# Attention and a selective scan on one core: the product with B on VectorE, the sum over states in quarters of the array

## The chip, the core and the metric

The kernel runs on one core of one Trainium2 chip. The core has a TensorE (matrix products, written to PSUM), a VectorE, a ScalarE (functions such as Exp), a GpSimd and 16 DMA engines fed by queues, among them that of SyncE. Each engine works through its own instructions in order, and semaphores hold one back until what it reads is there. The metric is the device time of the whole program in microseconds; lower is better.

## What is computed

The input x has 16 images of 256 channels and 32 x 32 positions, in float32. Two layers follow each other, each added to its input.

- The first normalizes in 16 groups, adds a position embedding, and runs self-attention over the 1024 positions with 4 heads of 32, then a feed-forward step.
- The second normalizes again and computes from 256 channels an inner u of 512 channels, with a gate z, and per position 64 values B and 64 values C. Its core is a recurrence over the 1024 positions, for each of 512 channels and 64 states:

```
dA = exp(delta * A)              # delta: [512, 1024], A: [512, 64]
h  = dA * h + (delta * u) * B    # one h for each channel and state
y  = sum over the 64 states of h * C
```

  Then y + u * D is multiplied by silu(z), projected to 256 channels, and multiplied by a sigmoid gate from a convolution over three positions.

There are 16 x 512 x 64 recurrences of 1024 steps, and every one is computed in full.

## The kernel before

The 512 channels of the scan are 4 blocks of 128, so channels lie on partitions and positions along the row. 16 images with 4 blocks each make 64 blocks of 64 states. `scan_layer` runs them one after the other. For each state n it

1. copies row n of B and row n of C from DRAM to all 128 partitions (tiles bt and ct, two buffers each, issued by SyncE, L429 and L430),
2. multiplies du = delta * u by bt on GpSimd into dub (four buffers, L432),
3. computes the decays da = exp(delta * A) on ScalarE in two halves of 512 positions, into two PSUM buffers (L436),
4. runs the recurrence on VectorE, half by half, in place in dub; the second half starts from the last element of the first (L440),
5. multiplies by ct on VectorE (L443),
6. sums over states on TensorE: a product with the identity that adds dub to y in PSUM, in two halves (L445). A float32 product appears in the trace as two passes, each with its own load of weights.

After the 64 states, y is taken from PSUM on VectorE (L455), the z products and silu follow (L462 to L470), and the next block begins with `deltas` (L397 to L416): a product, then a softplus in which ScalarE and VectorE take turns, then du.

Everything else is side work for the neighbouring images: the attention of the next one and the inputs of its scan, the gate and output of the last one. They are generators, and after every second state `scan_layer` takes one step of them (L450). Only the first image's attention and inputs run ahead of the first scan. `query_key` makes queries and keys for one head. In the attention of a head the scores are made twice: once to find the row maxima (L268, with a VectorE maximum of each at L271), and once transposed, with the maximum as an extra row, for Exp and the product with V (L290, L294, L295).

A scheduler orders the instructions of each engine from its own estimate of their durations and from priorities in the order of the program; the program's order is therefore not quite the engine's. Buffers come from pools: a tile with so many buffers waits, when it comes round again, for the last reader of the old content. PSUM has 8 banks: three for products of all kinds (mm), one for the attention's result (accp), two for y, two for the decays.

Of the kernel before, what the change touches and what calls it, by code (L numbers as in the profile page):

```python
# [10 lines left out]
F32 = mybir.dt.float32  # L11
AF = mybir.ActivationFunctionType
ALU = mybir.AluOpType
AX = mybir.AxisListType
PSUM = bass.MemoryType.PSUM
DRAM = bass.MemoryType.DRAM

P = 128
C = 256
KC = C // P  # L20
# [26 lines left out]
def attention_then_scan_kernel(  # L47
# [21 lines left out]
    def pool(name, bufs, **kw):  # L69
        return ctx.enter_context(tc.tile_pool(name=name, bufs=bufs, **kw))  # L70
# [9 lines left out]
    ptp = pool("ptp", 3)  # L80
    small = pool("small", 2)
    scan = pool("scan", 2)
    dubs = pool("dubs", 4)
    bcd = pool("bcd", 2, space=DRAM)
    mm = pool("mm", 3, space=PSUM)
    accp = pool("accp", 1, space=PSUM)
    yps = pool("yps", 1, space=PSUM)
    daps = pool("daps", 2, space=PSUM)


    vec = const.tile([P, NV], F32, name="vec")
# [2 lines left out]
    def col(name, i=0, n=1):  # L94
        o, w = _COLS[name]
        assert i + n <= w
        return vec[:, o + i : o + i + n]
# [21 lines left out]

    ident = const.tile([P, P], F32, name="ident")  # L120
    make_identity(nc, ident)
    avg = const.tile([P, P], F32, name="avg")
    nc.vector.memset(avg, 1.0 / C)
    eps = const.tile([P, 1], F32, name="eps")
# [5 lines left out]
    def psum(name, dims=P):  # L130
        return mm.tile([P, HL], F32, name=name, tag="mm")[:dims]
# [4 lines left out]
    def hwork(name):  # L136
        return half.tile([P, HL], F32, name=name, tag="half")

    def hs(h):
        return ts(h, HL)  # L140
# [69 lines left out]
    def attention_layer(b):  # L210
# [32 lines left out]
            yield  # L243


        def query_key(h):
            qa, ka = work("qa"), work("ka")
            for hf in range(2):
                ps = psum("qk_ps", 2 * DH)
                for k in range(KC):  # L250
                    nc.tensor.matmul(  # L251
                        ps, wqk_s[:, k, ts(h, 2 * DH)], xn[k][:, hs(hf)],
                        start=(k == 0), stop=(k == KC - 1),
                    )
                nc.scalar.activation(qa[:DH, hs(hf)], ps[:DH], AF.Copy, scale=DH**-0.5)
                nc.scalar.copy(ka[:DH, hs(hf)], ps[DH:])
            nc.gpsimd.memset(ka[DH : DH + 1], 1.0)
            return qa, ka

        ao = sums = None  # L260
        for h in range(HEADS):
            qa, ka = query_key(h)
            yield
            mx = small.tile([P, NJ, 2], F32, name="mx", tag="mx")
            for c in range(NJ):
                for hf in range(2):
                    s = psum("s_ps")
                    nc.tensor.matmul(  # L268
                        s, qa[:DH, ts(c, P)], ka[:DH, hs(hf)], start=True, stop=True
                    )  # L270
                    nc.vector.tensor_reduce(mx[:, c, hf : hf + 1], s, AX.X, ALU.max)  # L271
                yield
            neg = small.tile([P, NJ], F32, name="neg", tag="neg")
            nc.vector.tensor_reduce(neg, mx, AX.X, ALU.max, negate=True)
            for hf in range(2):
                row = psum("row_ps", 1)
                for c in range(NJ // 2):
                    i = hf * (NJ // 2) + c
                    nc.tensor.matmul(
                        row[:, ts(c, P)], neg[:, i : i + 1], ident, start=True, stop=True  # L280
                    )
                nc.scalar.copy(qa[DH : DH + 1, hs(hf)], row)
            yield
            if h == 0:
                ao, sums = work("ao"), work("sums")
            for hf in range(2):
                av = accp.tile([P, HL], F32, name="av", tag="av")[: 2 * DH]
                for j in range(NJ):
                    s = psum("st_ps")
                    nc.tensor.matmul(  # L290
                        s, ka[: DH + 1, ts(j, P)], qa[: DH + 1, hs(hf)], start=True, stop=True
                    )
                    pt = ptp.tile([P, HL], F32, name="pt", tag="pt")
                    nc.scalar.activation(pt, s, AF.Exp)  # L294
                    nc.tensor.matmul(  # L295
                        av, vv[j // (NJ // 2)][:, j % (NJ // 2), h, :], pt,
                        start=(j == 0), stop=(j == NJ - 1),
                    )
                    if j % 2:
                        yield  # L300
                nc.scalar.copy(ao[ts(h, DH), hs(hf)], av[:DH])
                nc.scalar.copy(sums[ts(h, DH), hs(hf)], av[DH:])
            yield
        for hf in range(2):
            nc.vector.reciprocal(sums[:, hs(hf)], sums[:, hs(hf)])  # L305
# [89 lines left out]


    def deltas(b, d):  # L397
        delta = dels.tile([P, L], F32, name="delta", tag="delta", bufs=2)
        for hf in range(2):
            ps = psum("d_ps")  # L400
            nc.tensor.matmul(
                ps, wdt_s[:, ts(d, P)], state[b]["dt"][:, hs(hf)], start=True, stop=True
            )
            o = delta[:, hs(hf)]
            e, s, l = hwork("sp_e"), hwork("sp_s"), hwork("sp_l")
            nc.scalar.activation(e, ps, AF.Abs, bias=col("dt_b", d))
            nc.scalar.activation(e, e, AF.Exp, scale=-1.0)
            nc.vector.tensor_scalar(s, e, 1.0, None, ALU.add)
            nc.scalar.activation(l, s, AF.Ln)  # L409
            nc.vector.scalar_tensor_tensor(e, s, 1.0, e, ALU.subtract, ALU.subtract)  # L410
            nc.vector.tensor_tensor(l, l, e, ALU.subtract)
            nc.scalar.activation(o, ps, AF.Relu, bias=col("dt_b", d))  # L412
            nc.vector.tensor_tensor(o, o, l, ALU.add)
        du = dels.tile([P, L], F32, name="du", tag="du", bufs=2)
        nc.vector.tensor_tensor(du, delta, state[b]["us"][d], ALU.mult)
        return delta, du  # L416

# [2 lines left out]
    def scan_layer(b, side):  # L420
        us, rows = state[b]["us"], state[b]["rows"]
        for d in range(ND):
            blocks = (d,)
            delta, du = deltas(b, d)
            ys = [yps.tile([P, L], F32, name="y", tag="y")]
            for n in range(NS):
                bt = scan.tile([P, L], F32, name="bt", tag="bt")
                ct = scan.tile([P, L], F32, name="ct", tag="ct")
                nc.sync.dma_start(bt, rows[n : n + 1].partition_broadcast(P))  # L429
                nc.sync.dma_start(ct, rows[NS + n : NS + n + 1].partition_broadcast(P))  # L430
                dub = dubs.tile([P, L], F32, name="dub", tag="dub")
                nc.gpsimd.tensor_tensor(dub, du, bt, ALU.mult)  # L432
                at = d * NS + n
                for hf in range(2):
                    da = daps.tile([P, HL], F32, name="da", tag="da")
                    nc.scalar.activation(  # L436
                        da, delta[:, hs(hf)], AF.Exp, scale=a_neg[:, at : at + 1]
                    )
                    before = dub[:, HL - 1 : HL] if hf else 0.0
                    nc.vector.tensor_tensor_scan(  # L440
                        dub[:, hs(hf)], da, dub[:, hs(hf)], before, ALU.mult, ALU.add
                    )
                nc.vector.tensor_tensor(dub, dub, ct, ALU.mult)  # L443
                for hf in range(2):
                    nc.tensor.matmul(  # L445
                        ys[0][:, hs(hf)], ident, dub[:, hs(hf)],
                        start=(n == 0), stop=(n == NS - 1),
                    )
                if n % 2:
                    next(side, None)  # L450

            for i, d in enumerate(blocks):
                for hf in range(2):
                    u = us[d][:, hs(hf)]
                    nc.vector.scalar_tensor_tensor(  # L455
                        u, u, col("D", d), ys[i][:, hs(hf)], ALU.mult, ALU.add
                    )
            for d in blocks:
                for hf in range(2):
                    ps = psum("z_ps")  # L460
                    for k in range(KC):
                        nc.tensor.matmul(  # L462
                            ps, win_s[:, k, ds(DI + d * P, P)],
                            state[b]["xp"][:, k, ds(1 + hf * HL, HL)],
                            start=(k == 0), stop=(k == KC - 1),
                        )
                    z = hwork("z")
                    nc.scalar.activation(z, ps, AF.Silu)
                    u = us[d][:, hs(hf)]
                    nc.vector.tensor_tensor(u, u, z, ALU.mult)  # L470


    def gate_and_store(b):
# [103 lines left out]
```

## Time and profile before

| | |
|---|---|
| median of 2 runs | 21276.39 us (21272.64 and 21280.14) |
| the profiled execution: time, span | 21280.14 us, 21278.3 us |
| TensorE busy, granted clock | 75%, 0.847 |
| VectorE busy | 91% |
| ScalarE busy | 41% |
| GpSimd busy | 50% |
| DMA | 4366 MB, 205 GB/s |

"Busy" is the time in which an engine runs an instruction, its waiting for a port inside the instruction included. A group row of the profile gives line, engine, operation, tiles, shapes and count, then busy time in us and the mean duration of one in ns, then the idle time of the engine just before these instructions and what ended most of it. A row of the timeline gives start and duration in us, engine, line, operation and count; x2 means that two instructions in a row are merged. PEld is TensorE's load of weights, which runs beside its products.

### The profile page before, as it was taken

To read this page: it belongs to the slowest core of one execution; us is meant where nothing else is said; L and a number is where in the kernel's file an instruction comes from. 1 tells how busy PE (TensorE), PEld (TensorE's weight loads), DVE (VectorE), ACT (ScalarE), POOL (GpSimd) and SP (SyncE) were. 2 spreads that over 40 slices of the span, in tenths; PEclk is the share of its full clock that TensorE was granted. 3 is DMA by queue.
4 is the path that set the end of the run, shared out by engine and by line. 5 is a ranking of instruction groups with operands and counts; after the bars stand their busy time and mean duration, and the time that the engine had idled before them with its cause. 6 is when DMAs were issued, how large, how long until landed. Compare 5 with 4: busy or idle time off the path is not lost.

```text
span 21278.3 us, 126145 instructions
## 1 busy us (share of the span) xinstructions
PE 15872.9 (75%) x30080; PEld 5818.2 (27%) x30080; DVE 19310.4 (91%) x15491; ACT 8732.8 (41%) x12360; POOL 10710.9 (50%) x4486
## 2 busy tenths in 40 slices
PE   8877868777687776877768777786777868778656
PEld 2222222232322323222222222322223222232212
DVE  4998998989989899898999989999998998989998
ACT  3443444434444344443444434444444344434433
POOL 1554554555545455555555455555554554545554
PEclk7888888888888888888888888888888888888878
DMA  1666656666666666666666566665665656656666
GB/s 64 215 211 203 219 199 207 212 201 214 206 211 209 200 213 205 212 204 203 213 208 215 201 208 213 207 217 201 213 204 201 224 200 206 208 203 223 202 221 210
DMA packets 1199439, 4366.25 MB, mean 205 GB/s; under 512 B 132817, under 2 KB 135249, under 8 KB 1198689
## 3 DMA queue, kind: packets, MB, share of 16 engines
q1 hardware_dynamic: 1182816, 4299.45, 60.4%
q0 software_dynamic: 15872, 58.73, 0.7%
q8 instruction: 236, 3.87, 0.1%
q14 instruction: 515, 4.21, 0.1%
HBM read 4332.47 MB, written 25.17 MB: 205 GB/s over the span
## 4 chain that ended last, share of the span: by engine, by line
DVE 41%; issue 22%; DMA 9%; PE 7%; ACT 6%; POOL 6%; DVEq 0%; SPq 0%; POOLq 0%; ACTq 0%
DVE dub L440 27%; DVE dub L443 10%; POOL dub L432 6%; DMA bt<-rows 5%; DMA ct<-rows 4%; PE y L445 4%; ACT da L436 3%; PE av L295 1%; DVE u L370 1%; DVE xn L204 0%; PE st_ps L290 0%; ACT L436 0%; DVE sums L305 0%; DVE xn L205 0%; ACT L409 0%
## 5 line engine op out<-in xcount | busy, mean ns | idle before, releaser
L432 POOL TENSOR_TENSOR dub<-du,bt 128x1024 f32<-128x1024 f32 x4096 | 10393.4, 2544 | 9821.0 <-DMA bt<-rows 4216.4
L445 PE MATMUL y<-dub,ident 128*128 128x512 f32 x16384 | 10075.2, 752 | 4576.3 <-DVE dub L443 4568.0
L440 DVE TENSOR_TENSOR_SCAN dub<-da,dub 128x512 f32<-128x512 f32 x8192 | 10070.1, 1241 | 956.9 <-POOL dub L432 705.4
L436 ACT ACTIVATE da<-delta,a_neg 128x512 f32<-128x512 f32 x8192 | 5642.5, 691 | 10511.2 <-DVE dub L440 10499.4
L443 DVE TENSOR_TENSOR dub<-dub,ct 128x1024 f32<-128x1024 f32 x4096 | 7095.2, 1734 | 110.7 <-DMA ct<-rows 66.0
L445 PEld LDWEIGHTS y<-dub,ident 128*128 128x128 f32 x16384 | 3424.0, 228 | 10665.2 <-DVE dub L443 7546.2
L268 PE MATMUL s_ps<-ka,qa 32*128 32x512 f32 x2048 | 1188.0, 688 | 129.1 <-DVE mx L271 127.9
L295 PE MATMUL av<-pt,vv 128*64 128x512 f32 x2048 | 1180.2, 682 | 134.6 <-ACT pt L294 134.6
L290 PE MATMUL st_ps<-qa,ka 33*128 33x512 f32 x2048 | 1104.2, 643 | 36.8 <-ACT delta L412 26.8
L294 ACT ACTIVATE pt<-st_ps 128x512 f32<-128x512 f32 x1024 | 593.8, 594 | 755.7 <-PE st_ps L290 751.9
L271 DVE TENSOR_REDUCE mx<-s_ps 128x1 f32<-128x512 f32 x1024 | 680.5, 665 | 210.3 <-PE s_ps L268 209.4
L268 PEld LDWEIGHTS s_ps<-ka,qa 32*128 32x128 f32 x2048 | 362.8, 204 | 971.4 <-issue 401.9
L290 PEld LDWEIGHTS st_ps<-qa,ka 33*128 33x128 f32 x2048 | 336.4, 192 | 781.1 <-issue 716.7
L295 PEld LDWEIGHTS av<-pt,vv 128*64 128x64 f32 x2048 | 242.4, 151 | 1024.0 <-ACT da L436 446.2
L482 PEld LDWEIGHTS g_ps<-wg_s,xp 128*128 128x128 f32 x1536 | 395.2, 327 | 80.2 <-issue 51.8
L482 PE MATMUL g_ps<-wg_s,xp 128*128 128x256 f32 x1536 | 408.3, 413 | 4.1 <-ACT delta L412 4.1
L436 ACT ACT_TABLE_LOAD x299 | 383.6, 1283 | 5.2
L370 DVE SCALAR_TENSOR_TENSOR u<-up,vec,u 128x1024 f32<-128x1024 f32 x192 | 319.7, 1672 | 7.5 <-ACT u L364 7.3
L493 PE MATMUL m_ps<-wo_s,u 128*128 128x256 f32 x1024 | 280.6, 418 | 33.6 <-DVE u L470 33.6
L197 PE MATMUL ln_v<-ln_sq,avg 128*128 128x512 f32 x256 | 167.4, 757 | 182.8 <-ACT ln_sq L196 182.8
L384 PE MATMUL x_ps<-u,wx_s 128*128 128x512 f32 (+1 forms) x512 | 279.4, 651 | 23.8 <-ACT u L376 23.7
L251 PE MATMUL qk_ps<-xn,wqk_s 128*64 128x512 f32 x512 | 284.8, 659 | 0.0
(111 smaller groups left out, 6881.3 us busy)
## 6 DMA issues: line engine op xcount, KB each, us to landing
bt<-rows SPq DMA_DIRECT2D x4096, 512.0 KB, 4.8
ct<-rows SPq DMA_DIRECT2D x4096, 512.0 KB, 4.2
X<-in_x_dram POOLq DMA_DIRECT2D x16, 1024.0 KB, 6.9
tok<-in_pos_dram POOLq DMA_DIRECT2D x32, 512.0 KB, 6.6
out_dram<-X POOLq DMA_DIRECT2D x32, 512.0 KB, 5.2
rows<-bc POOLq DMA_DIRECT2D x16, 512.0 KB, 3.9
win_s<-in_w_in_dram SPq DMA_DIRECT2D x1, 1024.0 KB, 14.9
wg_s<-in_w_gate_dram SPq DMA_DIRECT2D x1, 768.0 KB, 16.4
```

The source lines that it names most:

```text
L268: nc.tensor.matmul(s, qa[:DH, ts(c, P)], ka[:DH, hs(hf)], start=True, stop=True)
L271: nc.vector.tensor_reduce(mx[:, c, hf : hf + 1], s, AX.X, ALU.max)
L290: nc.tensor.matmul(s, ka[: DH + 1, ts(j, P)], qa[: DH + 1, hs(hf)], start=True, stop=True)
L294: nc.scalar.activation(pt, s, AF.Exp)
L295: nc.tensor.matmul(av, vv[j // (NJ // 2)][:, j % (NJ // 2), h, :], pt, start=(j == 0), stop=(j == NJ - 1),)
L370: nc.vector.scalar_tensor_tensor(u, up[:, t : t + L], col("conv_w", d * CONV + t), u, ALU.mult, ALU.add)
L432: nc.gpsimd.tensor_tensor(dub, du, bt, ALU.mult)
L436: nc.scalar.activation(da, delta[:, hs(hf)], AF.Exp, scale=a_neg[:, at : at + 1])
L440: nc.vector.tensor_tensor_scan(dub[:, hs(hf)], da, dub[:, hs(hf)], before, ALU.mult, ALU.add)
L443: nc.vector.tensor_tensor(dub, dub, ct, ALU.mult)
L445: nc.tensor.matmul(ys[0][:, hs(hf)], ident, dub[:, hs(hf)], start=(n == 0), stop=(n == NS - 1),)
L482: nc.tensor.matmul(ps[:, ts(q, C)], st["xp"][:, k, ds(first + t, P, 4)], wg_s[:, k, t, :], start=(i == 0), stop=(i == 3 * KC - 1),)
```

## The change

- The product with B goes from GpSimd to VectorE, from du and bt into hh, a tile with four buffers.
- The decays go to SBUF, whole, in one ScalarE instruction of 1024; the scan is one instruction of 1024, the product with C as before.
- The sum over states is made for two states at once, in 64 x 64 quarters of TensorE's array: eight products, of two channel halves i and two states j, and two halves of positions. Channel half i of state j is added to y4[i], partitions 64j on. At the end of a block ScalarE copies the four parts of y4 to SBUF, and a product with `fold` (two 64 x 64 identities above each other, in one half of the columns) adds both states' parts and puts the channel halves in place.
- PSUM: the decays' two banks go to the second y tile.
- The buffers of delta and du go from two to one.
- The attention takes two heads at a time: their queries and keys lie at partitions 0 and 64, and their products with V write the two halves of the rows of one PSUM bank. A step of the side work is again two score products, or two score products and two products with V.

```diff
+    fold = const.tile([P, 2, P], F32, name="fold")
+    nc.vector.memset(fold, 0.0)
+    for i in range(2):
+        for j in range(2):
+            nc.vector.tensor_copy(
+                fold[ts(j, 64), i, ts(i, 64)], ident[ts(j, 64), ts(j, 64)]
+            )
...
             for c in range(NJ):
                 for hf in range(2):
-                    s = psum("s_ps")
-                    nc.tensor.matmul(
-                        s, qa[:DH, ts(c, P)], ka[:DH, hs(hf)], start=True, stop=True
-                    )
-                    nc.vector.tensor_reduce(mx[:, c, hf : hf + 1], s, AX.X, ALU.max)
-                yield
+                    for e in range(2):
+                        r = ds(2 * DH * e, DH)
+                        s = psum("s_ps")
+                        nc.tensor.matmul(
+                            s, qa[r, ts(c, P)], ka[r, hs(hf)], start=True, stop=True
+                        )
+                        nc.vector.tensor_reduce(mx[:, e, c, hf : hf + 1], s, AX.X, ALU.max)
+                    yield
...
                 for j in range(NJ):
...
+                    pts = []
+                    for e in range(2):
+                        r = ds(2 * DH * e, DH + 1)
+                        s = psum("st_ps")
+                        nc.tensor.matmul(
+                            s, ka[r, ts(j, P)], qa[r, hs(hf)], start=True, stop=True
+                        )
+                        pt = ptp.tile([P, HL], F32, name="pt", tag="pt")
+                        nc.scalar.activation(pt, s, AF.Exp)
+                        pts.append(pt)
+                    for e in range(2):
+                        nc.tensor.matmul(
+                            av[ts(e, 2 * DH)],
+                            vv[j // (NJ // 2)][:, j % (NJ // 2), 2 * pair + e, :], pts[e],
+                            start=(j == 0), stop=(j == NJ - 1),
+                        )
+                    yield
...
-        delta = dels.tile([P, L], F32, name="delta", tag="delta", bufs=2)
+        delta = dels.tile([P, L], F32, name="delta", tag="delta", bufs=1)
...
-        du = dels.tile([P, L], F32, name="du", tag="du", bufs=2)
+        du = dels.tile([P, L], F32, name="du", tag="du", bufs=1)
...
-            ys = [yps.tile([P, L], F32, name="y", tag="y")]
+            y4 = [yps.tile([P, 2, HL], F32, name="y", tag=f"y{i}") for i in range(2)]
+            hhs = []
             for n in range(NS):
...
-                dub = dubs.tile([P, L], F32, name="dub", tag="dub")
-                nc.gpsimd.tensor_tensor(dub, du, bt, ALU.mult)
+                da = scan.tile([P, L], F32, name="da", tag="da")
                 at = d * NS + n
+                nc.scalar.activation(da, delta, AF.Exp, scale=a_neg[:, at : at + 1])
+                hh = scan.tile([P, L], F32, name="hh", tag="hh", bufs=4)
+                nc.vector.tensor_tensor(hh, du, bt, ALU.mult)
+                nc.vector.tensor_tensor_scan(hh, da, hh, 0.0, ALU.mult, ALU.add)
+                nc.vector.tensor_tensor(hh, hh, ct, ALU.mult)
+                hhs.append(hh)
+                if n % 2 == 0:
+                    continue
                 for hf in range(2):
-                    da = daps.tile([P, HL], F32, name="da", tag="da")
-                    nc.scalar.activation(
-                        da, delta[:, hs(hf)], AF.Exp, scale=a_neg[:, at : at + 1]
+                    for j in range(2):
+                        for i in range(2):
+                            nc.tensor.matmul(
+                                y4[i][ts(j, 64), hf, :], ident[ts(i, 64), ts(i, 64)],
+                                hhs[j][ts(i, 64), hs(hf)],
+                                start=(n == 1), stop=(n == NS - 1),
+                            )
+                hhs = []
+                next(side, None)
+
+            for hf in range(2):
+                y = psum("y_ps")
+                for i in range(2):
+                    t = hwork("yq")
+                    nc.scalar.copy(t, y4[i][:, hf, :])
+                    nc.tensor.matmul(y, fold[:, i, :], t, start=(i == 0), stop=(i == 1))
+                u = us[d][:, hs(hf)]
+                nc.vector.scalar_tensor_tensor(u, u, col("D", d), y, ALU.mult, ALU.add)
...
-                    before = dub[:, HL - 1 : HL] if hf else 0.0
-                    nc.vector.tensor_tensor_scan(
-                        dub[:, hs(hf)], da, dub[:, hs(hf)], before, ALU.mult, ALU.add
-                    )
-                nc.vector.tensor_tensor(dub, dub, ct, ALU.mult)
-                for hf in range(2):
-                    nc.tensor.matmul(
-                        ys[0][:, hs(hf)], ident, dub[:, hs(hf)],
-                        start=(n == 0), stop=(n == NS - 1),
-                    )
-                if n % 2:
-                    next(side, None)
```

## The prediction

> **What bounds the kernel now.** I read the head of the page first, then the chain that ended last, then the costliest groups, then the timeline of a few states.
>
> ```profile
> span 21278.3 us, 126145 instructions
> PE 15872.9 (75%) x30080; PEld 5818.2 (27%) x30080; DVE 19310.4 (91%) x15491; ACT 8732.8 (41%) x12360; POOL 10710.9 (50%) x4486
> ...
> DVE 41%; issue 22%; DMA 9%; PE 7%; ACT 6%; POOL 6%; DVEq 0%; SPq 0%; POOLq 0%; ACTq 0%
> ...
> L432 POOL TENSOR_TENSOR dub<-du,bt 128x1024 f32<-128x1024 f32 x4096 | 10393.4, 2544 | 9821.0 <-DMA bt<-rows 4216.4
> ...
> L440 DVE TENSOR_TENSOR_SCAN dub<-da,dub 128x512 f32<-128x512 f32 x8192 | 10070.1, 1241 | 956.9 <-POOL dub L432 705.4
> L436 ACT ACTIVATE da<-delta,a_neg 128x512 f32<-128x512 f32 x8192 | 5642.5, 691 | 10511.2 <-DVE dub L440 10499.4
> L443 DVE TENSOR_TENSOR dub<-dub,ct 128x1024 f32<-128x1024 f32 x4096 | 7095.2, 1734 | 110.7 <-DMA ct<-rows 66.0
> ```
>
> VectorE is busy 91% of the span and the decays on ScalarE wait 10499 us for it: VectorE sets the pace. Its multiplication by C (L443) averages 1734 ns. The timeline shows what it costs when nothing holds it:
>
> ```profile
> 8003.31 2.38 DVE L440 TENSOR_TENSOR_SCAN dub<-da,dub 128x512 f32<-128x512 f32 x2
> ...
> 8004.17 0.34 PEld L445 LDWEIGHTS y<-dub,ident 128*128 128x128 f32 x1 [0.43 <-issue]
> ...
> 8005.02 0.34 PEld L445 LDWEIGHTS y<-dub,ident 128*128 128x128 f32 x1 [0.52 <-issue]
> 8005.61 1.20 DVE L443 TENSOR_TENSOR dub<-dub,ct 128x1024 f32<-128x1024 f32 x1
> ...
> 8006.73 2.39 DVE L440 TENSOR_TENSOR_SCAN dub<-da,dub 128x512 f32<-128x512 f32 x2
> ...
> 8011.07 0.19 PEld L445 LDWEIGHTS y<-dub,ident 128*128 128x128 f32 x1 [0.24 <-issue]
> 8011.50 0.19 PEld L445 LDWEIGHTS y<-dub,ident 128*128 128x128 f32 x1 [0.24 <-issue]
> ```
>
> From start to start: the product by C takes 8006.73-8005.61 = 1.12 us, two half scans 8005.61-8003.31 = 2.30 us. I sorted all 4096 executions of L443 by whether a GpSimd product (L432) runs beside them: 1202 without have a median of 1.20 us, 2894 with have a mean of 1.96 us. So GpSimd's product costs VectorE about 0.5 us a state, and VectorE's 91% hold this waiting.
>
> Per block of 64 states (64 blocks), from the first scan to the last product by C, the timeline gives 306.1 us on average: 285 to 289 in the last three blocks, which have no side work, 291 and 292 in blocks 1 and 2 of an image, 320 and 321 in blocks 0 and 3. Between blocks lies a gap of 19.5 us. First scan at 427, last product at 21244: 427 + 64 x 306.1 + 63 x 19.5 + 34 = 21280, which is the span.
>
> **What the Trainium skill says.** "SBUF — State Buffer", section "SBUF: two separate sides": the port pair shared by VectorE and GpSimd is an exclusive lock, against VectorE instructions with two SBUF inputs; the loser blocks. The trace agrees: L443 (two SBUF inputs) goes from 1.20 to 1.96 us, the scan, whose decays lie in PSUM, stays at 1.24 with and without GpSimd. "DVE: opcode table, instruction layouts, handler registers and perf-mode slots", section "Datapath and trigger behaviour": the scan runs at half throughput. It agrees: 512 elements of scan take what 1024 of a product take. "TensorEngine Tiling (Array Packing)", "Key Properties": tiles of the array work independently, in parallel. No run here shows it yet. "TensorE: Matmul & The Clock Gate", Part 1: TensorE's clock is halved when it is little active. It agrees: the weight loads of passes of 512 columns are 0.43 us apart at 8011, 0.85 at 8004.
>
> **The change, part by part.**
>
> *Product with B moves to VectorE.* Added: 4096 products of 128x1024, the shape of L443, at 1.12 us. Removed: GpSimd's lock, so that L443 falls to 1.12 too. If L443 stayed at 1.73 for another cause this would be +5000 us; the free executions exclude that.
>
> *Scan whole, decays in SBUF.* Two elements' time per element, so twice the product's 1.067 us of streaming plus its fixed 0.05: 2.18 us; the halves as measured, 2.30. In the changed kernel's order two states' steps interleave (scan, scan, product, product), so no step waits for the one before it. I take 2.20. Now with two SBUF inputs, it meets no GpSimd product.
> A state: 1.12 + 2.20 + 1.12 = 4.44 us; 64 make 284 us (283 to 290). Against 285 to 289 now without side work: nothing is won or lost here. What the lock cost is what the new product costs.
>
> *The side work becomes visible.* Now it costs blocks 1 and 2 only 4 us, as GpSimd gets ahead meanwhile and blocks less. Afterwards each VectorE instruction of it adds its whole time. At uncontended start-to-start times (1024 maxima at 0.58 = 596; 192 at L370 at 1.19 = 228; the norms, copies and gates) it sums to 2270 us; 550 of it belong to the gaps (L408 to L415, L455, L470). 1720 x 15/16 (the first image's lies ahead of the blocks) / 64 = 25 us a block, less 2 that the order puts into gaps. Waits inside a block are 15.6 us now, 11.0 of them (705/64) on GpSimd, which go; 5 stay. Body: 284 + 23 + 5 = 312 us, against 306.1.
>
> *The gap.*
>
> ```profile
> 9557.99 1.23 DVE L443 TENSOR_TENSOR dub<-dub,ct 128x1024 f32<-128x1024 f32 x1
> 9563.09 1.41 DVE L455 SCALAR_TENSOR_TENSOR u<-u,vec,y 128x512 f32<-128x512 f32 x2 [3.87 <-PE y L445]
> ...
> 9576.81 1.22 DVE L440 TENSOR_TENSOR_SCAN dub<-da,dub 128x512 f32<-128x512 f32 x1 [1.38 <-POOL dub L432]
> ```
>
> Now: 9576.81 - 9559.22 = 17.6 us here, with half of the next deltas already begun. Added: at the end TensorE has 6 quarter products left (7 overlapped passes, 3 us), then four copies on ScalarE (0.58 each) and four folds (two passes each, 3.4), then z (8 passes, 3.4), and only then the deltas' products (1.7). With ScalarE's chain behind it (Abs, Relu, a table load of 1.28, Exp, a load, Ln, twice, 10 us) and VectorE's last steps I get 24 us at the full clock, 34 at half. The deltas' buffers go from two to one; both are free by then, so that alone costs nothing. A third at half clock: 27 us. Bounds 22 and 34.
>
> *Sum over states in quarters.* Now 4 products a pair of states, 8 passes, 3.4 us at full clock. Afterwards 8, 16 passes. If a pass starts as soon as its quarter is free, each product's second pass runs beside the next one's first, and the pair takes 8 slots, 3.4 us again; with no overlap 6.9, with all four at once 1.7. I take 3.4: within the 8.9 us of VectorE's pair it is hidden, beside 2.3 us of side products (13696 other passes, 4700 us at full clock, over 2048 pairs). If that cover goes, VectorE waits at the product with B for one of the four hh buffers, and the scan behind it too.
>
> *Transfers.* Two B rows are now asked for after two products with B, two C rows after two products with C. Each has 7.7 us until needed; the second of two transfers issued together lands after 4.9 us in the median, 6.4 at the 99th percentile of all. Hidden. ScalarE's exponentials (one of 1024, 1.06 us as at L171, for two of 0.69) are hidden too.
>
> *Attention in halves.* Ahead of the first scan, from 100 to 300 us, the windows show TensorE busy for 196.4 of 200 us, so overlap shows there alone: up to 125 us of 250, at least 0. I take 87: 427 becomes 340. In the blocks attention stands beside the scan. The copies into qa and ka double in number, not on the path.
>
> *Sum:* 340 + 64 x 312 + 63 x 27 + 34 = 22043, about **22050 us**, 3.6% over the profiled execution's 21280.1 (4 us over the median of 21276.4, so the same for the median).
>
> **The rivals.**
> 1. *TensorE comes late at times.* Quarters count as little activity, the clock halves, and an attention pair costs 6.9 + 6 = 12.9 us against VectorE's 10. Some 1100 such pairs, a third to all of them slow: 1100 to 3200 us more: 22500 to 24500. For it: TensorE was at half clock a third of the time. Against: blocks 1 and 2 bear 13.8 us of half-clock passes a pair today and lose 4 us.
> 2. *Quarters don't overlap.* 16 + 5 passes a pair: 9.2 us at full clock, 18.3 at half; at the mean clock of 0.847 10.9, so 340 + 2048 x 10.9 + 63 x 35 + 34 = 24900; 24500 to 37000.
> 3. *Other side: the gap is covered.* If the next block's deltas and the side work filled the gaps to VectorE's own 8.6 us, and waits in blocks vanished: 340 + 64 x 307 + 63 x 8.6 + 34 = 20560, 3.4% faster. No change at a gap of 20; 2% faster from 13 down. Against it: in the changed order every product with B of the next block stands behind its deltas, and these behind z. A cheaper mix (gap 22, no waits) ends at 21400.
>
> **How the numbers follow.** Main case 0.60, its own range 21650 to 22500; rival 1 0.15; rival 2 0.08; rival 3 with its partial forms 0.17, of it 0.03 beyond 2%. A difference under 2% cannot be told from none. The likeliest is 22050. The range leaves out rival 2, the top of rival 1 and the bottom of rival 3: 21500 to 23700. Faster 0.03; same (20851 to 21702) 0.17; slower 0.80.
>
> **What would show it.** Right: products with B and C near 1.2 us each, scans near 2.25; VectorE 93% busy or more; last blocks' bodies 283 to 290 us; gaps 24 to 30; body means over 306; first scan near 340. Wrong: a large idle time of the product with B put down to TensorE (rivals 1, 2); passes of quarters 0.43 us apart with no overlap (rival 2); gaps under 20 (rival 3); scans far from 2.2 us.

## The result and the profile after

The changed kernel takes 21915.65 us (median of 2 runs, 21909.69 to 21921.62) against 21276.39 us before: a ratio of 1.03, 95% interval 1.0256 to 1.0345. It is slower by 3%. The forecast was 22050 us.

The page of the changed kernel, its head, its chain and its costliest VectorE groups:

```profile
span 21907.9 us, 147098 instructions
...
PE 13839.0 (63%) x46720; PEld 4399.5 (20%) x46720; DVE 20688.6 (94%) x15464; ACT 7687.4 (35%) x8360; POOL 502.4 (2%) x390
...
DVE 31%; issue 29%; DMA 23%; PE 4%; ACT 4%; POOL 0%; DVEq 0%; ACTq 0%; POOLq 0%
...
L459 DVE TENSOR_TENSOR_SCAN hh<-da,hh 128x1024 f32<-128x1024 f32 x4096 | 9239.9, 2293 | 0.1
...
L458 DVE TENSOR_TENSOR hh<-du,bt 128x1024 f32<-128x1024 f32 x4096 | 4866.9, 1226 | 3.9 <-PE y L467 3.1
L460 DVE TENSOR_TENSOR hh<-hh,ct 128x1024 f32<-128x1024 f32 x4096 | 4844.6, 1220 | 0.1
```

GpSimd has gone from 50% to 2%, and the product with C from 1734 to 1220 ns. But VectorE has 4096 products more and is busy 94%. Inside a block it now hardly waits: the idle times ahead of the three groups add to 4.1 us in the whole span. A pair of states in the timeline:

```profile
11655.93 4.47 DVE L459 TENSOR_TENSOR_SCAN hh<-da,hh 128x1024 f32<-128x1024 f32 x2
...
11660.32 2.34 DVE L460 TENSOR_TENSOR hh<-hh,ct 128x1024 f32<-128x1024 f32 x2
...
11661.58 4.41 PE L467 MATMUL y<-hh,ident 64*64 64x512 f32 x16 [4.09 <-DVE hh L460]
11662.57 2.36 DVE L458 TENSOR_TENSOR hh<-du,bt 128x1024 f32<-128x1024 f32 x2
...
11664.84 4.47 DVE L459 TENSOR_TENSOR_SCAN hh<-da,hh 128x1024 f32<-128x1024 f32 x2
```

From scan to scan 8.91 us, 4.455 us a state, with each of the three steps of VectorE end to end. The sixteen passes of quarters fit in beside. The gap between two blocks, as VectorE sees it:

```profile
9776.24 2.35 DVE L460 TENSOR_TENSOR hh<-hh,ct 128x1024 f32<-128x1024 f32 x2
9784.58 0.75 DVE L482 SCALAR_TENSOR_TENSOR u<-u,vec,y_ps 128x512 f32<-128x512 f32 x1 [5.99 <-PE y_ps L480]
9786.29 0.75 DVE L482 SCALAR_TENSOR_TENSOR u<-u,vec,y_ps 128x512 f32<-128x512 f32 x1 [0.97 <-PE y_ps L480]
9789.98 1.29 DVE L494 TENSOR_TENSOR u<-u,z 128x512 f32<-128x512 f32 x2 [2.94 <-ACT z L492]
9794.08 0.43 DVE L431 TENSOR_SCALAR sp_s<-sp_e 128x512 f32<-128x512 f32 x1 [2.81 <-ACT sp_e L430]
...
9804.25 3.44 DVE L458 TENSOR_TENSOR hh<-du,bt 128x1024 f32<-128x1024 f32 x2
```

From the end of the last product with C (9778.59) to the first product of the next block are 25.7 us. Taken over the whole timeline, in us:

| | before | changed | difference |
|---|---|---|---|
| start of the first scan (product) | 427.0 | 348.4 | -78.6 |
| a block of 64 states, mean of 64 | 306.06 | 308.63 | 64 x 2.57 = +164 |
| the last three blocks, without side work | 284.6 to 289.3 | 285.1 | |
| a gap, mean of 63 | 19.51 | 27.72 | 63 x 8.21 = +517 |
| after the last block | 34.4 | 60.5 | +26 |
| span | 21278.3 | 21907.9 | +629 |

So most of the loss lies in the gaps, and little in the blocks.

### The profile page after: what moved, and what is told of

The parts are those of the page before. It is cut to its first block, busy times and chain, and to the rows that moved or that the text cites. A ratio compares the mean times of both kernels' runs of the same rounds, so it can differ in the third digit from the quotient of the medians.

```text
span 21907.9 us, 147098 instructions
## 1 busy us (share of the span) xinstructions
PE 13839.0 (63%) x46720; PEld 4399.5 (20%) x46720; DVE 20688.6 (94%) x15464; ACT 7687.4 (35%) x8360; POOL 502.4 (2%) x390
## 4 chain that ended last, share of the span: by engine, by line
DVE 31%; issue 29%; DMA 23%; PE 4%; ACT 4%; POOL 0%; DVEq 0%; ACTq 0%; POOLq 0%
DMA ct<-rows 19%; DVE hh L460 12%; DVE hh L459 9%; DVE hh L458 6%; DMA bt<-rows 3%; DVE mx L285 2%; PE y L467 2%; PE y_ps L480 1%; PE z_ps L486 1%; ACT L430 1%; DMA X<-in_x_dram 0%; ACT L432 0%; DVE xn L210 0%; DVE u L393 0%; ACT sp_e L430 0%
## 5 line engine op out<-in xcount | busy, mean ns | idle before, releaser
L467 PE MATMUL y<-hh,ident 64*64 64x512 f32 x32768 | 8599.8, 931 | 7229.2 <-DVE hh L460 7214.6
L459 DVE TENSOR_TENSOR_SCAN hh<-da,hh 128x1024 f32<-128x1024 f32 x4096 | 9239.9, 2293 | 0.1
L456 ACT ACTIVATE da<-delta,a_neg 128x1024 f32<-128x1024 f32 x4096 | 4693.2, 1148 | 11804.0 <-DVE hh L459 11774.4
L467 PEld LDWEIGHTS y<-hh,ident 64*64 64x64 f32 x32768 | 2263.4, 189 | 13049.9 <-DVE hh L460 10743.1
L458 DVE TENSOR_TENSOR hh<-du,bt 128x1024 f32<-128x1024 f32 x4096 | 4866.9, 1226 | 3.9 <-PE y L467 3.1
L460 DVE TENSOR_TENSOR hh<-hh,ct 128x1024 f32<-128x1024 f32 x4096 | 4844.6, 1220 | 0.1
L316 PE MATMUL av<-pt,vv 128*64 128x512 f32 x2048 | 926.2, 660 | 171.6 <-ACT pt L313 168.3
L282 PE MATMUL s_ps<-ka,qa 32*128 32x512 f32 x2048 | 922.8, 808 | 50.5 <-DVE mx L285 50.1
L309 PE MATMUL st_ps<-qa,ka 33*128 33x512 f32 x2048 | 854.4, 641 | 0.0
L480 PE MATMUL y_ps<-yq,fold 128*128 128x512 f32 x512 | 264.5, 663 | 43.4 <-ACT yq L479 43.4
```

The source lines that it names most:

```text
L282: nc.tensor.matmul(s, qa[r, ts(c, P)], ka[r, hs(hf)], start=True, stop=True)
L309: nc.tensor.matmul(s, ka[r, ts(j, P)], qa[r, hs(hf)], start=True, stop=True)
L316: nc.tensor.matmul(av[ts(e, 2 * DH)], vv[j // (NJ // 2)][:, j % (NJ // 2), 2 * pair + e, :], pts[e], start=(j == 0), stop=(j == NJ - 1),)
L456: nc.scalar.activation(da, delta, AF.Exp, scale=a_neg[:, at : at + 1])
L458: nc.vector.tensor_tensor(hh, du, bt, ALU.mult)
L459: nc.vector.tensor_tensor_scan(hh, da, hh, 0.0, ALU.mult, ALU.add)
```

## The experiments

The theory: VectorE alone sets the pace. A block loses GpSimd's lock and gains a product; the gap grows by the copies and folds that the quarters need. The rivals: TensorE (quarters, half clock) holds the blocks back; or the rows of B and C do. A block is taken from its first scan (in the changed kernel: its first product with B) to its last product with C, and a gap lies between two blocks. Below, a time with an interval beside it is the median of four runs, and one without is a single run; the runs of the kernel before lay between 21145 and 21291 us.

### The sum in the whole array again

```diff
-                                y4[i][ts(j, 64), hf, :], ident[ts(i, 64), ts(i, 64)],
-                                hhs[j][ts(i, 64), hs(hf)],
-                                start=(n == 1), stop=(n == NS - 1),
+                        y[:, hs(hf)], ident, hh[:, hs(hf)], start=(n == 0), stop=(n == NS - 1),
...
-                    nc.scalar.copy(t, y4[i][:, hf, :])
-                    nc.tensor.matmul(y, fold[:, i, :], t, start=(i == 0), stop=(i == 1))
```

> The changed kernel with the sum over states in the whole array again, one state at a time, added to one y tile that VectorE reads directly; no copies, no folds. Theory (the time is lost in the gaps between blocks and in uncovered side work, TensorE is hidden): bodies stay at 307 to 310 us, gaps fall from 27.7 to 20 to 22 us, so about 21450 us (21400 to 21550). Rival (the quarters and TensorE's half clock hold VectorE back inside the blocks): bodies shorten by 5 us or more, under 21150 us. If the quarters are what keeps TensorE ahead, bodies lengthen instead and the time stays over 21700 us.

Measured: 21464.86 us, ratio to the kernel before 1.0094 (1.0077 to 1.011). Gaps 19.8 us, blocks 309.6 us, last three 285.1 us. The quarters cost 8.0 us a gap and nothing in a block: they are 2.1 of the 3.0%, and TensorE holds no block back, in either form. TensorE's rows in the timeline, first of this kernel,

```profile
21164.06 6.77 PE L461 MATMUL y<-hh,ident 128*128 128x512 f32 x8 [2.80 <-DVE hh L459]
```

against 4.41 us for the sixteen passes above, both at half clock (whole-array passes 0.85 us apart): the quarters do save TensorE time, where it isn't needed.

### Without the product with B, in both kernels

In the changed kernel:

```diff
-                nc.vector.tensor_tensor(hh, du, bt, ALU.mult)
-                nc.vector.tensor_tensor_scan(hh, da, hh, 0.0, ALU.mult, ALU.add)
+                nc.vector.tensor_tensor_scan(hh, da, bt, 0.0, ALU.mult, ALU.add)
```

> The changed kernel without the product with du: the scan reads the row of B itself, so this part of the computation is left out. Theory (VectorE alone sets the pace of a block): 64 x 1.13 = 72 us less a block, bodies near 236 us, gaps as they are, about 17270 us. Rival (rows of B and C come no faster than now): they are asked for 1.05 MB in 3.3 us, 315 GB/s, where now 199 GB/s take 59% of the DMA engines, so a transfer limit would show as waits of VectorE for bt or ct and a time over 18000 us.

Measured: 18588.32 us, blocks 256.4 us where the theory said 236. In the kernel before:

```diff
-                nc.gpsimd.tensor_tensor(dub, du, bt, ALU.mult)
...
-                        dub[:, hs(hf)], da, dub[:, hs(hf)], before, ALU.mult, ALU.add
+                        dub[:, hs(hf)], da, bt[:, hs(hf)], before, ALU.mult, ALU.add
```

> The kernel before without GpSimd's product: the scan reads the row of B from bt and writes dub, so this part of the computation is left out. Theory (the lock that GpSimd takes is what the kernel before pays in a block): the product by C falls from 1.73 to 1.2 us on average, a state takes 3.4 to 3.75 us, bodies near 250 us, about 17600 us (16900 to 18300). Rival (GpSimd's product was hidden beside VectorE and something else held the pace of 4.45 us a state): bodies stay over 280 us, over 19500 us.

Measured: 18685.11 us, blocks 274.7 us, gaps 10.3 us, the product with C 1223 ns. That is over the theory's range and under the rival's. The lock is there, and its removal shows in the product with C:

```profile
L442 DVE TENSOR_TENSOR dub<-dub,ct 128x1024 f32<-128x1024 f32 x4096 | 5010.2, 1223 | 101.7 <-DMA ct<-rows 13.5
```

Both kernels came out over what the theory said. One part of it is that VectorE now waits for rows of B. A line of VectorE's waits from each (us in total, times, longest), the changed kernel first:

```profile
DVE hh L458 <- DMA bt<-rows: 490.2, 968, 1.8
```

```profile
DVE dub L439 <- DMA bt<-rows: 330.5, 714, 2.6
```

The rows land hardly later than before (4.9 us after they are asked for, in the median of both; 4.8 in the kernel before, 5.6 in the changed one), so the likely reason is that two buffers are too few at this pace; no run tested it alone. But these waits are 8 and 5 us a block, and the blocks are 20 and 25 us over. Another part in the changed kernel is the order: without its product a state's scan and product with C often follow each other directly, and each costs more when it waits for the instruction just before it (a scan between two products 2.33 us from start to start, where it was 2.20). The rival of the rows thus shows at some 4 us a state, not at 4.45.

With these floors under both, the product costs 21915 - 18588 = 3327 us on VectorE and 21276 - 18685 = 2591 us on GpSimd: on GpSimd it was far from free, but still cheaper. Of the 2591 us, 2006 lie in the blocks and 577 in the gaps; why the gaps shorten by 9 us, no run shows.

### The product with B back on GpSimd, decays left in SBUF

```diff
-                nc.vector.tensor_tensor(hh, du, bt, ALU.mult)
+                nc.gpsimd.tensor_tensor(hh, du, bt, ALU.mult)
```

> The changed kernel with the product with B back on GpSimd; decays stay in SBUF, so the scan has two SBUF inputs. Theory (the lock holds against every VectorE instruction with two SBUF inputs, the scan too): a state is 2.2 + 1.13 us of VectorE after 2.4 us of GpSimd, 5.7 us, so bodies near 385 us and about 27000 us (25500 to 28500), scans well over 2.3 us on average. Rival (only the products meet GpSimd, the scan doesn't): bodies of 306 us or less, under 21900 us.

Measured: 25908.02 us, blocks 369.1 us. The groups of this kernel:

```profile
L458 POOL TENSOR_TENSOR hh<-du,bt 128x1024 f32<-128x1024 f32 x4096 | 13188.4, 3228 | 11655.0 <-DMA bt<-rows 5267.2
...
L459 DVE TENSOR_TENSOR_SCAN hh<-da,hh 128x1024 f32<-128x1024 f32 x4096 | 12550.1, 3077 | 929.9 <-POOL hh L458 927.4
...
L460 DVE TENSOR_TENSOR hh<-hh,ct 128x1024 f32<-128x1024 f32 x4096 | 8669.2, 2128 | 116.6 <-DMA ct<-rows 64.9
```

The scan goes from 2293 to 3077 ns: with its decays in SBUF it meets the lock, as the theory said. The 3298 scans that run beside a product of GpSimd take 3272 ns on average, the 798 others 2271. So decays in SBUF are dear while the product is on GpSimd. The opposite half, the product on VectorE with the decays left in PSUM, was not run, so how the cost of the two moves divides is not shown.

### Attention two heads at once, alone

The kernel before with the attention of the changed one (`query_key` by pairs and the loop over pairs, as in the diff above).

> The kernel before with the attention two heads at once as its one change. Theory (it helps only where TensorE is the bound, ahead of the first scan): first scan from 427 to about 348 us, bodies and gaps within 2 us of before, so 79 us less, about 21195 us (21150 to 21240). Rival (it changes the blocks too, since its steps put more of TensorE or ScalarE between the decays): bodies move by more than 3 us on average, so the time moves by 200 us or more either way.

Measured: 20783.34 us, ratio 0.9791 (0.9754 to 0.9829). First scan at 351, as expected; but blocks fall from 306.1 to 302.0 us and gaps from 19.5 to 17.5. The rival was right: in the kernel before this change reaches into the blocks. By what wait it does so, no run shows. The reverse, in the changed kernel:

> The changed kernel with the attention one head at a time again as its one edit. In the kernel before, two heads at once took 2.1% off, of which only 76 us lay ahead of the first scan. Theory (with VectorE's work uncovered, the order of the side work hardly matters in the blocks): first scan near 427 us again, bodies and gaps within 1.5 us of the changed kernel, so 80 to 200 us more, about 22040 us. Rival (two heads at once help the blocks here as much as in the kernel before): 400 us or more on top, over 22300 us.

```diff
-        for pair in range(HEADS // 2):
-            qa, ka = query_key(pair)
+        for h in range(HEADS):
+            qa, ka = query_key(h)
```

(with the rest of the attention as it was before). Measured: 22113.57 us, ratio 1.0402 (1.0385 to 1.0419): 198 us more than the changed kernel, first scan at 426, blocks 2.7 us longer, gaps 0.5 shorter. The time is within the theory's range, at its upper end, but the blocks moved by more than its 1.5 us: blocks and gaps together are some 120 us, not none.

Put in a row, each against the kernel before: attention in pairs 0.979; product and decays moved as well 1.0094; quarters as well 1.03. In this order the change is a gain of 2% and two losses of 3 and 2%. The order matters: taken off the changed kernel, the attention in pairs is worth 1%.

### When GpSimd holds the lock

Why does GpSimd's product cost so much in the kernel before? I sorted its starts by their distance from the end of the last product with C. The first guess was late rows of B:

```diff
-                bt = scan.tile([P, L], F32, name="bt", tag="bt")
+                bt = scan.tile([P, L], F32, name="bt", tag="bt", bufs=3)
...
-    dubs = pool("dubs", 4)
+    dubs = pool("dubs", 5)
...
-        delta = dels.tile([P, L], F32, name="delta", tag="delta", bufs=2)
+        delta = dels.tile([P, L], F32, name="delta", tag="delta", bufs=1)
```

(and du likewise.)

> The kernel before with three buffers for the rows of B and five for dub in place of two and four; delta and du have one buffer each to make the room. Theory (GpSimd's product begins late in the scan because its row of B comes late, and so still holds the lock when the product with C is due): the product with C falls from 1.73 to under 1.5 us, bodies to about 260 us, about 18500 us (17500 to 19900). Rival (SyncE's queue holds a row of B behind a row of C that waits for VectorE, whatever the buffers): bodies stay at 295 us or more, over 20600 us.

Measured: 21293.06 us, blocks 305.6 us, product with C 1828 ns: nothing gained, as the rival said. With the rows of C on ScalarE's queue besides (`nc.scalar.dma_start(ct, ...)`):

> As the kernel with three buffers for the rows of B and five for dub, and the rows of C are asked for by ScalarE's queue, so that a row of B stands behind no wait for VectorE. Theory: GpSimd runs ahead, its products fall beside the scans, a state takes 2.4 + 1.1 to 3.9 us, bodies 240 to 265 us, about 18000 us (17300 to 19300), and the product with C falls under 1.4 us. Rival (two engines that share the lock can't be kept apart by earlier rows): the product with C stays over 1.6 us, and the time over 20500 us.

Measured: 21850.16 us, blocks 314.9 us, slower, and the rival's numbers again. Now the rows are early, and GpSimd waits for something else:

```profile
POOL dub L432 <- PE y L445: 7698.6, 2615, 11.7
```

It runs ahead until its buffers are used up, and then starts whenever TensorE gives one back: 2.6 us in the median after the end of a product with C. As it takes 2.4 us itself and a state 4.9, it often still runs when the next one is due. Half of the products on each engine:

```diff
-                nc.gpsimd.tensor_tensor(dub, du, bt, ALU.mult)
+                (nc.vector if n % 2 else nc.gpsimd).tensor_tensor(dub, du, bt, ALU.mult)
```

> The kernel before with every second product with B on VectorE, the others on GpSimd. Theory (a product on VectorE costs its own 1.12 us; one on GpSimd costs up to 1.0 us through lock and lateness, but less where GpSimd has two states' time for one product): bodies 275 to 295 us, about 20200 us (19500 to 20900). Rival (the exchange is even, each product costs the same on either engine): bodies near 306 us, 21200 to 21500 us.

Measured: 22747.09 us, blocks 325.4 us, worse than either kernel and outside both the theory's range and the rival's. Its groups:

```profile
L443 DVE TENSOR_TENSOR dub<-dub,ct 128x1024 f32<-128x1024 f32 x4096 | 6093.2, 1488 | 28.0 <-DMA ct<-rows 21.7
...
L432 DVE TENSOR_TENSOR dub<-du,bt 128x1024 f32<-128x1024 f32 x2048 | 3791.8, 1851 | 19.0 <-PE y L445 13.6
```

VectorE's own products, 1.2 us when alone, take 1.49 and 1.85. Per pair of states that is 2 x 0.27 + 0.63 = 1.2 us for one product on GpSimd, more than the 1.12 that VectorE would need to make it. So this mixture saves nothing.

Next, the product with C writes a tile of its own, so that dub comes free with that product and not with TensorE's sum (attention in pairs included; TensorE sums w):

```diff
-                nc.vector.tensor_tensor(dub, dub, ct, ALU.mult)
+                w = dubs.tile([P, L], F32, name="w", tag="w")
+                nc.vector.tensor_tensor(w, dub, ct, ALU.mult)
```

> The kernel before with the attention two heads at once, and with the product with C written to a tile of its own, w (three buffers), in place of dub (now three buffers; delta and du one each). So a buffer of dub comes free when VectorE has finished the product with C, not when TensorE has summed it, and GpSimd's next product can begin right then, beside the scan, which needs no lock. Theory (in the kernel before GpSimd always waits for something that comes 1.4 us or more after the product with C, and then still holds the lock when the next one is due): the product with C falls from 1.73 to under 1.5 us and bodies from 302 to under 275 us: 17500 to 19300 us. If rows of B come too late for that, as they are asked for behind rows of C: half of it, 19300 to 20300 us. Rival (the contention doesn't depend on when GpSimd's product starts): 20600 us or more.

Measured: 20301.14 us, ratio 0.9564 (0.9548 to 0.958), blocks 293.7 us: at the end of the theory's lesser case. Against the kernel with attention in pairs alone, 20783 us, it is 2% faster. GpSimd waits 4872 us for rows of B. With both mended, rows of C on ScalarE's queue, three buffers for rows of B, two for dub:

> As the kernel with w, with dub two buffers, rows of B three, and the rows of C asked for by ScalarE's queue, so that a row of B waits for GpSimd alone. Theory (start of GpSimd's product right after the product with C): a state takes 3.5 to 3.9 us, bodies 240 to 265 us, the product with C under 1.35 us, about 18000 us (17300 to 19300). Rival (the contention doesn't depend on when GpSimd's product starts, or ScalarE's queue holds the decays back behind a row of C): 20600 us or more.

Measured: 19138.29 us, ratio 0.9017 (0.9004 to 0.9031), blocks 275.6 us, 246 without side work. The time is within the theory's range, the blocks are 10 us over it. The product with C, and a state in the timeline of this kernel:

```profile
L460 DVE TENSOR_TENSOR w<-dub,ct 128x1024 f32<-128x1024 f32 x4096 | 5105.2, 1246 | 331.8 <-DMA ct<-rows 47.5
```

```profile
18701.90 1.23 DVE L460 TENSOR_TENSOR w<-dub,ct 128x1024 f32<-128x1024 f32 x1
18703.04 2.60 DVE L456 TENSOR_TENSOR_SCAN dub<-da,dub 128x512 f32<-128x512 f32 x2
...
18703.26 2.35 POOL L448 TENSOR_TENSOR dub<-du,bt 128x1024 f32<-128x1024 f32 x1 [1.49 <-DVE w L460]
...
18705.73 1.22 DVE L460 TENSOR_TENSOR w<-dub,ct 128x1024 f32<-128x1024 f32 x1
```

GpSimd's product starts 0.13 us after the product with C has ended and is over before the next: a state takes 3.83 us. The kernels side by side; the last two hold the attention in pairs, so the second row is their base:

| | start of GpSimd's product after the last product with C, median us | products with C over 1.4 us | mean ns of a product with C | time us |
|---|---|---|---|---|
| before | 2.12 | 46% | 1734 | 21276 |
| before, attention in pairs | 1.87 | 48% | 1746 | 20783 |
| three rows of B, five dub, rows of C by ScalarE | 2.63 | 35% | 1828 | 21850 |
| w | 0.80 | 47% | 1660 | 20301 |
| w, and rows in time | 0.13 | 3% | 1246 | 19138 |

GpSimd makes the same 4096 products in all five. In the last kernel only 136 products with C still run beside one of them, where 2900 did in its base, and a product with C is 0.5 us shorter on average. So the cost of the shared port depends here on when GpSimd starts. Earlier rows alone did not bring this (third row), and the buffer w alone only in part. This kernel beats both.

## Why the prediction was right

*A state, 4.44 us; bodies without side work 283 to 290.* Measured 4.455 us and 285.1. The product's 1.12 was 1.13 us from start to start, the scan's 2.20 was 2.19. "Nothing is won or lost here" holds for the blocks without side work: 285.1 against 284.6 to 289.3. The reason given for it, "what the lock cost is what the new product costs", does not. In the last three blocks of the kernel before a state of 4.49 us is 2.50 for the two half scans, 1.75 for the product with C and 0.22 of waits. The lock is thus some 0.6 us of the 1.14 that the new product costs. Half scans that wait for each other give another 0.3, as one whole scan takes 2.20, and the waits 0.2. The prediction took its 2.30 for the halves from a stretch where the steps of two states alternate (the product with C at 8005.61 starts before the scan ahead of it has ended). So the forecast of the new state stands by its own sum, and this account of the old one was wrong in its parts.

*Side work visible.* Body 312 forecast, 308.6 measured: of the three terms, the waits were mis-sized, 1.2 us a block measured where 5 were taken. With the attention in pairs and the sum in the whole array on both sides, side work costs 302.0 - 284.9 = 17 us a block under GpSimd's product and 309.6 - 285.1 = 24.5 us without it. That it would come into view was right.

*The gap, 27 us.* Measured 27.7; 8.0 us of it are the quarters' copies and folds, by the run without them. The other two changes nearly cancel in the gap: attention in pairs took 2.0 us off, the move of product and decays put 2.3 on.

*Quarters hidden.* Right, and with more room than reckoned: mostly 4.4 to 4.8 us a pair at half clock, and 1.9 to 3.1 at full clock where 3.4 were taken, so more passes overlap than was assumed. VectorE waited for TensorE at the product with B once, 3.1 us. The premise of rival 1 came true, half clock for 52% of the time instead of a third, and had no effect on the blocks; rival 2's 13.7 us at half clock did not occur.

*Attention in halves.* 87 us ahead of the first scan forecast, 78.6 measured. The step "in the blocks attention stands beside the scan", which gave it no worth there, failed: 120 us in the changed kernel by the run with one head at a time, and 350 to 390 us in blocks and gaps of the kernel before (by the medians and by the two profiles).

*The end.* Taken as 34 us as before; it was 60.5. From 21850 us on, TensorE still has 180 passes to do, where the kernel before had 79 from 21245 on: more of the last image's gate is left over. The step left out that the order of side work changes at the end too.

In sum -216 us for the blocks, +46 for the gaps, +8 at the start, +26 at the end: 136 of the 22043 were too many. Part of this closeness is that the errors have opposite signs; all of one sign, they would have been 296 us, still inside the main case's own range.

## What to carry to other kernels

Before an operation is moved off a busy engine, or back, price what its old place really costs: here GpSimd's product cost 2591 us, most of it (4096 x 0.51 = 2093 us) in longer products with C, and on VectorE it cost 3327. Where two engines share a port, look at when the second one starts; making it start right after the first's last instruction of two SBUF inputs (by the buffer that releases it, with its rows in time) was worth 8% against the same kernel without (19138 against 20783 us), with the same work. And a form that relieves an engine with time to spare (TensorE) can cost what it adds between blocks, where VectorE waits for it.

## What the runs showed of the hardware that was not expected

The two passes of one 64 x 64 quarter start 7 ns apart in the trace, and sixteen of them begin within 3.8 us at half clock (2973.09 to 2976.84), where whole-array passes need 0.85 us each. The prediction had let a product's second pass wait for its first.

TensorE's clock stood at half for three quarters of the quarters' passes, though TensorE was busy 63% of the span; with the same sum in the whole array its mean went from 0.741 to 0.827. Nor does being busy alone bring the full clock in the kernel before: from 54.1 to 81.4 us TensorE is busy for 26.2 of 27.3 us, with attention's scores of 32 rows as most of its work, and the clock is half all through, while from 81.4 to 118.9 us, with scores and products of 128 rows by turns, it is full. Whether the part of the array in use decides it, no run tested alone.

```profile
54.10:81.40 27.30, 26.22 (x44) 10.31 (x43) 9.94 (x16) 0.73 (x2) 0.00 (x0) 0.50 0.00 1
```

(This row of a table by window gives the stretch and its length, then busy time and count of TensorE, its weight loads, VectorE, ScalarE and GpSimd, then the clock, the DMA share and GB/s.)

A second half scan that starts from the first one's last element begins 1.32 us after the start of the first when nothing else lies between, in the median of 2961 such pairs of the fastest kernel (the two of 18703.04 take 2.60 us in all). Where the next instruction need not wait for it, a half scan of the kernel before takes as little as 1.115 us from start to start. One scan of 1024 in the changed kernel takes 2.20. The same 1.32 us stand in the kernel before without GpSimd's product, so GpSimd is not the cause; the 0.2 us are the price of waiting for the instruction just before.
